# Gathering 14 columns a layer for fewer partitions, with VectorE filling in the rest

## The chip, the cores and the metric

The kernel runs on one core of a Trainium2 chip. The metric is device time in microseconds of one execution; the figure given for a kernel is the median of its runs. A profile is one execution of its own, taken by the hardware profiler, and its times are its own.

## What is computed

A graph with 6250 nodes and 100,000 edges (sorted by destination) goes through two GATv2 layers and one GAT layer, each followed by what the listing shows; features are 256 wide. In all three, a node gathers one row from each of its sources, turns them to logits, takes a softmax over its own edges and adds up the weighted rows.

```python
def _gatv2_layer(x, src, dst, n, Wl, Wr, att, b):      # H, C = 4, 64; edges have self-loops added
    xl = (x @ Wl).reshape(n, H, C)
    xr = (x @ Wr).reshape(n, H, C)
    e = leaky_relu(xl[src] + xr[dst], 0.2)
    logits = einsum('ehc,hc->eh', e, att)
    alpha = segment_softmax(logits, dst)
    out = segment_sum(xl[src] * alpha[:, :, None], dst, num_segments=n)
    return out.reshape(n, H * C) + b

h = elu(_gatv2_layer(x, ..., first weights))
x = layernorm(x + _gatv2_layer(h, ..., second weights))
Wh = einsum('nf,hfd->hnd', x, W)                       # 8 heads of 32
e = leaky_relu(s1[:, src] + s2[:, dst], 0.2)
attn = segment_softmax(e, dst)
x = layernorm(x + segment_sum(attn[:, :, None] * Wh[:, src], dst))
```

(`segment_softmax` stands for the maximum, exponential, sum and division that the reference writes out.)

## The kernel before

**Plan.** `make_plan` (L715) counts each node's edges, sorts the nodes by that number, most first, and cuts them into 49 blocks of 128 nodes, one node to a partition. Node r of the order is partition r mod 128 of block r // 128. `columns` (L46) works out from the sizes alone how many columns each block gets: `cols` is 38 for block 0 (27 of them held in the block, the rest by a special path called "few"), then 25, 24, 23, 22, 21, 21, 20 and so on down to 9 for block 48, such that a node of block b has more than `cols[b]` edges only with a chance that is neglected. `near` holds for each node the list of its sources, with a place NP for "no source" where the list is shorter than the columns; row NP of each table has logits of -1.5e38 or rows that lead to them (`nobody`). The tile `most` (L926) holds the number of columns of each block; L1163 compares the counts with it, and a graph that doesn't fit goes by `tile_general_path` (L81), a slower program in the same kernel. The rows of layer 1's table are written by the plan as well.

**Layers.** `tile_by_degree` (L1208) does the three layers. `layer2` (L1536) is called twice for the GATv2 layers, and the GAT layer stands open at the end (from L1758). For each block, in order:

- `gather_rows` (L1295) issues one indirect DMA from GpSimd's queue for each column: 128 rows of the table, one to a partition, by the indices of that column (L1300). They land in tiles `g` of at most 9 columns. There are 9 such tiles (L1266), and a block takes two or three, four at block 0. In layers 1 and 2 column 0 of a block's tiles is the node's own row and comes from elsewhere.
- `attend` (L1576) has VectorE take the maximum with the own right-hand row `xr` (L1591, or `first_z` at L1567 for the first tile of the next block), the product with the attention vector (L1594) and the sum over each head (L1595), which gives `lg`. `weights` (L1434) takes VectorE's maximum over the columns (L1439), ScalarE's exponential with its sum (L1446), and VectorE's division (L1451, L1452).
- `weighted_sum` (L1464) multiplies the gathered rows by the weights, most columns on VectorE (L1483) and the last ones on ScalarE (L1482), and lets TensorE add the columns up into `acc` (L1490).
- `finish1` and `finish2` make the next layer's rows and write them (L1708, L1709, L1740).
- In layer 3 `attend` (L1771) adds two numbers per edge (L1782), VectorE multiplies all columns by their weights (L1503) and adds them up (L1512), and the finished rows are scattered by GpSimd (L1812).

The program of each engine is written out in order by hand (no scheduler): for block b the gathers of block b+1 are issued first, then b+1's own rows are made ready, then `attend(b)`, then the finish of b-1 and the weighted sum of b.

**From one layer to the next.** `begin` (L1382) starts the next layer's gathers early: the first 14, 12 and 11 columns of blocks 0, 1 and 2 (`EARLY`), from indices in `soon`, as soon as the rows of blocks 0 to 44 of the new table are written. `sort_sources` (L1388) has put those blocks' sources in order in layer 1.

Of the kernel before, what the change touches and what calls it, by code (L numbers as in the profile page):

```python
# [35 lines left out]
P = 128  # L36
BIG = 1.5e38
SLOPE = 0.2
EPS = 1e-5
FAR = 1 << 20  # L40
RUNS = 64
EARLY = (14, 12, 11)
LATE = 4


def columns(E, N, NB):  # L46

    mean = E / N
    pmf = [math.exp(-mean)]
    for k in range(1, 200):
        pmf.append(pmf[-1] * mean / k)
    over, sd = [], []
    for c in range(199):
        p = sum(pmf[c + 1 :])
        g = sum((k - mean) * pmf[k] for k in range(c + 1, 200))
        over.append(N * p)  # L60
        sd.append(math.sqrt(max(N * (p * (1.0 - p) - g * g / mean), 0.0)))
    cols = []
    for b in range(NB):
        most = P * b
        cols.append(next(
            c for c in range(199) if (over[c] + 3.5 * sd[c] <= most if b else over[c] < 0.01)
        ))
    low = max((c for c in range(199) if N - over[c] <= P // 4), default=0)
    high = next(c for c in range(199) if over[c] <= P // 4)
    pmf += [0.0] * 200  # L70
    held = next(
        c for c in range(199)
        if N * sum((k - c) * pmf[k] for k in range(c, 200))
        + 3.5 * math.sqrt(N * sum((k - c) ** 2 * pmf[k] for k in range(c, 200))) <= P
    )
    assert cols[1] <= held < cols[0]
    return cols, low, high, held


@with_exitstack  # L80
# [565 lines left out]
@with_exitstack  # L646
def kernel(
    ctx: ExitStack,
    tc: tile.TileContext,
    x: bass.AP,  # L650
    src: bass.AP,
    dst: bass.AP,
    wl1: bass.AP,
    wr1: bass.AP,
    att1: bass.AP,
    b1: bass.AP,
    wl2: bass.AP,
    wr2: bass.AP,
    att2: bass.AP,
    b2: bass.AP,  # L660
    w3: bass.AP,
    a3: bass.AP,
    out: bass.AP,
):
    nc = tc.nc
    N, F = x.shape
    E = src.shape[0]
    NB = -(-N // P)
    NP = NB * P
    cols, low, high, held = columns(E, N, NB)  # L670
    CM = max(cols)
    H2, D2 = att1.shape
    H1 = w3.shape[0]
    W2 = H2 * (D2 + 1)

    dram = ctx.enter_context(tc.tile_pool(name="plan_dram", bufs=1, space=DRAM))
    plan = ctx.enter_context(tc.tile_pool(name="plan", bufs=1))
    node_i = plan.tile([P, NB], I32, name="node_i")
    fits = plan.tile([P, 1], I32, name="fits")
    done = plan.tile([P, 1], I32, name="done")  # L680
    ident = plan.tile([P, P], F32, name="ident")
    eps = plan.tile([P, 1], F32, name="eps")
    nobody = plan.tile([1, 2, max(W2 + 1, F + H1)], F32, name="nobody")
    att = [plan.tile([P, H2, D2 + 1], F32, name=f"att_r{i}") for i in range(2)]
    wc = [plan.tile([P, 2, 2, H2, D2 + 1], F32, name=f"wcat{i}") for i in range(2)]
    wh = plan.tile([P, 2, F + 2 * H1], F32, name="wh_cat")
    fixed = plan.tile([P, 4, F], F32, name="fixed_r")
    xl1_d = dram.tile([NP + 1, W2 + 1], F32, name="xl1_d")
    near_d = dram.tile([NP, CM + F], F32, name="near_d")

    with tc.manual_schedule():
        make_plan(
            tc, x, src, dst, ((wl1, wr1, att1), (wl2, wr2, att2)), (b1, b2), w3, a3,
            cols, low, high, held, node_i, fits, ident, eps, nobody, att, wc, wh, fixed, xl1_d, near_d,
        )
        nc.vector.memset(done, 0)

    att = [t.rearrange("p h d -> p (h d)") for t in att]
    wc = [w.rearrange("p j c h d -> p j c (h d)") for w in wc]
    ok = nc.values_load(fits[0:1, 0:1], min_val=0, max_val=1)  # L700
    with tc.If(ok != 0):
        with tc.manual_schedule():
            tile_by_degree(
                tc, x, att1, b1, b2, w3, a3, out, [held] + cols[1:], node_i, near_d, ident, eps, nobody,
                xl1_d, att, wc, wh, fixed, done,
            )
    right = nc.values_load(done[0:1, 0:1], min_val=0, max_val=1)
    with tc.If(right == 0):
        tile_general_path(
            tc, x, src, dst, wl1, wr1, att1, b1, wl2, wr2, att2, b2, w3, a3, out,  # L710
        )
# [1 line left out]

@with_exitstack
def make_plan(  # L715
    ctx, tc, x, src, dst, layers, biases, w3, a3, cols, low, high, held, node_i, fits, ident, eps, nobody,
    att, wc, wh, fixed, xl1_d, near_d,
):


# [1 line left out]
    nc = tc.nc  # L722
# [205 lines left out]
    for b in range(1, NB + 1):  # L928
        if b == NB or cols[b] != cols[b0]:
            nc.gpsimd.memset(most[:, b0:b], float(cols[b0]))  # L930
            b0 = b

# [271 lines left out]

@with_exitstack
def tile_by_degree(  # L1208
    ctx, tc, x, att1, b1, b2, w3, a3, out, cols, node_i, near_d, ident, eps, nobody,
    xl1_d, att, wc, wh, fixed, done,  # L1210
):
    nc = tc.nc
# [76 lines left out]
    def node(b):  # L1289
        return bass.IndirectOffsetOnAxis(ap=node_i[:, b : b + 1], axis=0)  # L1290

    def source(of, b, j):
        return bass.IndirectOffsetOnAxis(ap=of[:, b, j : j + 1], axis=0)

    def gather_rows(b, rows, cut, own, table, of, width, j0, j1):  # L1295


        for g, (s0, s1) in zip(rows, cut):
            for j in range(max(s0 - own, j0), min(s1 - own, j1)):
                nc.gpsimd.indirect_dma_start(  # L1300
                    out=g[:, j + own - s0, :width], out_offset=None, in_=table,
                    in_offset=source(of, b, j),
                )

    def find_few(work, ps):

# [229 lines left out]
    def layer2(i, table, of, width, start, own, finish, follow):  # L1536
# [5 lines left out]
        with ExitStack() as es:  # L1542
# [24 lines left out]
            def first_z(b):  # L1567
                rows, cut, xr = state[b]
                n = cut[0][1]
                z = zp.tile([P, T, W2], F32, name="z")[:, :n, :]  # L1570
                nc.vector.tensor_max(  # L1571
                    z, rows[0][:, :n, :W2], xr[:, None, :].to_broadcast([P, n, W2])
                )
                state[b].append(z)

            def attend(b):  # L1576
                rows, cut, xr, *made = state.pop(b)
                S = cols[b] + 1
                lg = work.tile([P, CM + 1, H2], F32, name="lg")
                if b == 0:  # L1580
                    own_r = work.tile([P, W2], F32, name="few_own", bufs=1)
                    nc.scalar.copy(own_r, xr)
                    po = pst.tile([P, W2], F32, name="few_r", tag="tp")
                    nc.tensor.matmul(po, node_of, own_r, start=True, stop=True)
                for g, (s0, s1) in zip(rows, cut):
                    n = s1 - s0
                    if s0 == 0 and made:
                        z = made[0]
                    else:
                        z = zp.tile([P, T, W2], F32, name="z")[:, :n, :]  # L1590
                        nc.vector.tensor_max(  # L1591
                            z, g[:, :n, :W2], xr[:, None, :].to_broadcast([P, n, W2])
                        )
                    nc.vector.tensor_mul(z, z, at[:, None, :].to_broadcast([P, n, W2]))  # L1594
                    nc.vector.reduce_sum(  # L1595
                        lg[:, s0:s1, :], z.rearrange("p t (h d) -> p t h d", h=H2), axis=AX.X
                    )
                if b == 0:
                    none(po)
                    z = zp.tile([P, T, W2], F32, name="z")[:, 0, :]  # L1600
                    nc.vector.tensor_max(z, few_row[:, :W2], po)
                    nc.vector.tensor_mul(z, z, at)
                    few_lg = work.tile([P, H2], F32, name="few_lg", bufs=1)
                    nc.vector.reduce_sum(few_lg, per_head(z, H2), axis=AX.X)
                    few_logits(work, pst, lg, few_lg, H2)
                    if i == 0:
                        nc.vector.tensor_copy(few_at[:, 1:], few_row[:, W2 : W2 + 1])
# [150 lines left out]
    with ExitStack() as es:  # L1758
# [12 lines left out]
        def attend(b):  # L1771
# [3 lines left out]
            if b == 0:  # L1775
                few_logits(work, ps, lg, few_row[:, F:A1], H1)
                nc.vector.tensor_add(
                    lg[:, cols[0] :, :], lg[:, cols[0] :, :],
                    s2[:, :1, :].to_broadcast([P, FEW, H1]),
                )  # L1780
            for g, (s0, s1) in zip(rows, cut):
                nc.vector.tensor_add(  # L1782
                    lg[:, s0:s1, :], g[:, : s1 - s0, F:A1],
                    s2[:, b : b + 1, :].to_broadcast([P, s1 - s0, H1]),
                )
            nc.vector.scalar_tensor_tensor(
                lg[:, :S, :], lg[:, :S, :], SLOPE, lg[:, :S, :], op0=OP.mult, op1=OP.max
            )
# [84 lines left out]
```

## Time and profile before

| | us |
|---|---|
| median of 3 runs | 3332.04 |
| lowest and highest of them | 3331.96, 3335.03 |
| the profiled execution, as timed | 3328.12 |
| its span in the profile | 3326.3 |
| VectorE busy | 2755.3 |
| GpSimd busy | 2435.2 |
| TensorE matmuls, weight loads busy | 1416.2, 1131.0 |
| ScalarE busy | 1108.0 |

The profile has 24,261 instructions in this span. The stages, read from its timeline: the plan until the first row gather at 131.25 us, layer 1 until VectorE's first product of layer 2 at 1261.70, layer 2 until its last row is written (issued at 2278.5), with layer 3's early gathers from 2235.97, then layer 3. The mean granted clock of TensorE is 0.711 of full speed.

How to read it: "busy" leaves out the time in which an engine's queue issues or waits, so that an engine can be full below 100%. A timeline row has the start, the duration, the engine, the line, the operation, the tile written and the tiles read, and, in brackets, how long the engine stood idle before it and what ended that; "issue" means that the profile shows nothing that it waited for. A group's row has its busy time and the mean duration in ns, then the idle time before its instructions. A row of waits has the total, the number and the longest. Rows by stretch have busy time and instruction count of each engine.

### The profile page before, as it was taken

The page shows a single profiled execution, that of the slowest core. Times are in us where ns is not written, and L with a number is a line of the kernel's source. Part 1 is how long each engine was busy: PE and PEld are TensorE (multiplying, and loading weights), DVE is VectorE, ACT ScalarE, POOL GpSimd, SP SyncE. Part 2 cuts the span into 40 slices and gives each one's busy share as a digit, 9 for nine tenths or more (in the row PEclk, how much of TensorE's full clock was granted, in tenths as well). Part 3 has the DMA queues.
Part 4 walks back from the last instruction along what each step waited for, and adds up shares of the span by engine and source line. Part 5 has one row for each costly group of instructions (what it writes and reads, how often), then busy time and mean ns, then how long its engine had stood idle before and what let it go on. Part 6 is the DMA issues. An engine that isn't in the chain of part 4 may idle for free.

```text
span 3326.3 us, 24261 instructions
## 1 busy us (share of the span) xinstructions
PE 1416.2 (43%) x5423; PEld 1131.0 (34%) x5424; DVE 2755.3 (83%) x2527; ACT 1108.0 (33%) x4428; POOL 2435.2 (73%) x2588
## 2 busy tenths in 40 slices
PE   7346666666677773565656666662000000000000
PEld 5235554555555552454545454552000000000000
DVE  7599998889888888999999999985966767666766
ACT  3134434444444442444445666561000000000000
POOL 5477777777777767777777777767777777777776
PEclk8678888888888886777877878886555555555555
DMA  8744444444444444444444444444333333333333
GB/s 198 145 111 118 117 118 121 118 120 122 121 121 121 124 111 112 122 121 127 121 127 126 132 126 132 131 111 115 108 107 107 108 108 107 108 107 107 107 107 86
DMA packets 189103, 395.84 MB, mean 119 GB/s; under 512 B 56249, under 2 KB 107963, under 8 KB 188934
## 3 DMA queue, kind: packets, MB, share of 16 engines
q0 software_dynamic: 121392, 339.19, 39.0%
q1 hardware_dynamic: 59858, 53.27, 5.7%
q10 hardware_dynamic: 7700, 1.74, 0.5%
q8 instruction: 47, 0.77, 0.1%
q14 instruction: 106, 0.87, 0.1%
HBM read 354.02 MB, written 40.42 MB: 119 GB/s over the span
## 4 chain that ended last, share of the span: by engine, by line
POOL 23%; DVE 15%; issue 13%; PE 7%; DMA 3%; ACT 1%; DVEq 0%; POOLq 0%; ACTq 0%
POOL g L1300 22%; PE acc L1490 6%; DVE g L1483 3%; DVE z L1594 3%; DVE lg L1595 3%; DVE z L1571 3%; DVE z L1591 2%; DMA g<-xl_d,near_r 1%; POOL out L1812 1%; DMA out<-y,node_i 1%; PE pm L1427 1%; DVE stats L1522 0%; DMA g<-whs_d,near_r 0%; ACT sd L1526 0%; DVE weighted L1503 0%
## 5 line engine op out<-in xcount | busy, mean ns | idle before, releaser
L1300 POOL DMA_INDIRECT g<-xl_d,near_r x1569 | 1484.4, 946 | 485.8 <-issue 434.8
L1490 PE MATMUL acc<-g,ident 128*128 128x256 f32 x3408 | 972.0, 455 | 654.2 <-DVE g L1483 357.6
L1490 PEld LDWEIGHTS acc<-g,ident 128*128 128x128 f32 x3408 | 788.8, 235 | 838.3 <-DVE g L1483 378.4
L1300 POOL DMA_INDIRECT g<-whs_d,near_r x766 | 727.1, 949 | 233.3 <-issue 227.2
L1482 ACT ACTIVATE g<-g,by 128x64 f32<-128x64 f32 x2308 | 561.0, 336 | 1.6
L1595 DVE TENSOR_REDUCE lg<-z 128x28 f32<-128x1820 f32 (+4 forms) x234 | 497.4, 2125 | 8.1
L1594 DVE TENSOR_TENSOR z<-z,at 128x1820 f32<-128x1820 f32 (+4 forms) x234 | 496.9, 2124 | 4.7
L1483 DVE TENSOR_TENSOR g<-g,wt 128x1792 f32<-128x1792 f32 (+8 forms) x234 | 331.8, 1435 | 31.9 <-ACT by L1473 31.9
L1512 DVE TENSOR_REDUCE acc_v<-weighted 128x256 f32<-128x4096 f32 (+15 forms) x49 | 343.7, 7014 | 1.6
L1591 DVE TENSOR_TENSOR z<-g,pr 128x1820 f32<-128x1820 f32 (+3 forms) x138 | 299.6, 2171 | 23.2 <-DMA g<-xl_d,near_r 14.8
L1456 ACT ACTIVATE wt<-lg 128x128 f32<-128x128 f32 (+17 forms) x49 | 14.0, 285 | 803.6 <-DVE lg L1455 803.6
L1782 DVE TENSOR_TENSOR lg<-g,s_r 128x56 f32<-128x56 f32 (+4 forms) x111 | 22.4, 214 | 268.5 <-DMA g<-whs_d,near_r 212.2
L1571 DVE TENSOR_TENSOR z<-g,pr 128x2080 f32<-128x2080 f32 (+4 forms) x96 | 197.9, 2061 | 44.5 <-DMA g<-xl_d,near_r 13.5
L1503 DVE TENSOR_TENSOR weighted<-g,wt 128x1792 f32<-128x1792 f32 (+4 forms) x111 | 226.6, 2057 | 0.1
L1422 ACT COPY xT<-pt 128x256 f32<-128x256 f32 x147 | 55.0, 374 | 505.8 <-PE pt L1420 505.8
L1446 ACT ACTIVATE wt<-lg,top 128x19 f32<-128x19 f32 (+14 forms) x392 | 115.7, 295 | 234.2 <-DVE top L1439 224.7
L1427 PE MATMUL pm<-wcat,xT 128*128 128x260 f32 x392 | 99.0, 395 | 22.6 <-ACT xT L1422 22.6
L1427 PEld LDWEIGHTS pm<-wcat,xT 128*128 128x128 f32 x392 | 70.4, 189 | 42.8 <-ACT xT L1422 34.3
L1446 ACT ACTIVATION_READ_ACCUMULATOR wt<-lg,top 128x1 f32 x392 | 73.5, 187 | 0.0
L1812 POOL DMA_INDIRECT out<-y,node_i x49 | 50.1, 1022 | 25.8 <-issue 14.2
L1427 PE MATMUL pm<-wh_cat,xT 128*128 128x272 f32 x196 | 59.0, 424 | 22.6 <-ACT xT L1422 22.6
L1427 PE MATMUL pl<-wcat,xT 128*128 128x260 f32 x196 | 57.2, 415 | 25.2 <-ACT xT L1422 25.2
(250 smaller groups left out, 1527.3 us busy)
## 6 DMA issues: line engine op xcount, KB each, us to landing
g<-xl_d,near_r POOLq DMA_INDIRECT x1569, 2.8
g<-whs_d,near_r POOLq DMA_INDIRECT x766, 2.8
whs_d<-row SPq DMA_DIRECT2D x49, 132.0 KB, 2.0
xl_d<-xl SPq DMA_DIRECT2D x49, 130.0 KB, 7.9
xl_d<-row SPq DMA_DIRECT2D x49, 130.0 KB, 2.6
xr_d<-row SPq DMA_DIRECT2D x49, 130.0 KB, 2.9
two<-xl_d SPq DMA_DIRECT2D x49, 130.0 KB, 2.9
two<-xr_d SPq DMA_DIRECT2D x49, 130.0 KB, 3.3
```

The source lines that it names most:

```text
L1300: nc.gpsimd.indirect_dma_start(out=g[:, j + own - s0, :width], out_offset=None, in_=table, in_offset=source(of, b, j),)
L1427: nc.tensor.matmul(pm, xT[:, c, :], w[:, c, :], start=c == 0, stop=c == 1)
L1446: nc.scalar.activation(wt[:, :, h], lg[:, :S, h], AF.Exp, bias=top[:, h : h + 1], accum_out=den[:, h : h + 1],)
L1482: nc.scalar.mul(g4[:, t, h, :], g4[:, t, h, :], by[:, t - m, h : h + 1])
L1483: nc.vector.tensor_mul(g4[:, :m], g4[:, :m], wt[:, s0 : s0 + m, :].unsqueeze(3).to_broadcast([P, m, H, F // H]),)
L1490: nc.tensor.matmul(acc, ident, g4[:, t], start=False, stop=s0 + t == S - 1 and not more)
L1503: nc.vector.tensor_mul(prod[:, s0 - base : s1 - base, :].rearrange("p t (h d) -> p t h d", h=H), g[:, :n, :F].rearrange("p t (h d) -> p t ...
L1512: nc.vector.reduce_sum(part, prod[:, : s1 - base, :].rearrange("p s f -> p f s"), axis=AX.X)
L1571: nc.vector.tensor_max(z, rows[0][:, :n, :W2], xr[:, None, :].to_broadcast([P, n, W2]))
L1591: nc.vector.tensor_max(z, g[:, :n, :W2], xr[:, None, :].to_broadcast([P, n, W2]))
L1594: nc.vector.tensor_mul(z, z, at[:, None, :].to_broadcast([P, n, W2]))
L1595: nc.vector.reduce_sum(lg[:, s0:s1, :], z.rearrange("p t (h d) -> p t h d", h=H2), axis=AX.X)
```

## The change

For each column c of a block b from 1 on, the same statistic that sets `cols` bounds how many nodes of the block can have more than c edges. Where that bound, rounded up to a multiple of 32, is 32, 64 or 96, the column is "short". There are 14 such columns: (block, column: rows) 1, 24: 64; 2, 23: 32; 3, 22: 64; 13, 18: 32; 17, 17: 64; 26, 15: 96; 31, 14: 96; 36, 13: 32; 40, 12: 32; 43, 11: 32; 45, 10: 96; 47, 9: 32; 48, 7: 96; 48, 8: 32. All but the first of block 48's are the last column of their block.

A short column is gathered for its first n partitions only. At the start of `attend(b)` VectorE writes zeros to the other partitions of that column of `g`, and after the logits are made it writes -1.5e38 to their logits. Partitions 32 to 127 take two such writes (32 to 63, and 64 to 127), partitions from 64 or from 96 on take one. In layer 1 blocks 0 to 2 are left as they were, since their columns also carry the sources that `sort_sources` needs; the early gathers use no short column. In the plan GpSimd writes the lower limits into `most` for those partitions, so that the comparison at L1163 covers them.

```diff
+QUARTER = 32
...
+    short = {}
+    for b in range(1, NB):
+        for c in range(cols[b]):
+            most = math.ceil((over[c] + 3.5 * sd[c] - P * b) / QUARTER) * QUARTER
+            if QUARTER <= most < P:
+                short[b, c] = most
+    return cols, low, high, held, short
+
+def past(n):
+    return ([(QUARTER, 2 * QUARTER)] if n == QUARTER else []) + [(max(n, 2 * QUARTER), P)]
...
+    for (b, c), n in sorted(short.items(), key=lambda e: -e[0][1]):
+        for p0, p1 in past(n):
+            nc.gpsimd.memset(most[p0:p1, b : b + 1], float(c))
...
     def gather_rows(b, rows, cut, own, table, of, width, j0, j1):
         for g, (s0, s1) in zip(rows, cut):
             for j in range(max(s0 - own, j0), min(s1 - own, j1)):
+                n = rows_of(b, j, width)
                 nc.gpsimd.indirect_dma_start(
-                    out=g[:, j + own - s0, :width], out_offset=None, in_=table,
-                    in_offset=source(of, b, j),
+                    out=g[:n, j + own - s0, :width], out_offset=None, in_=table,
+                    in_offset=bass.IndirectOffsetOnAxis(ap=of[:n, b, j : j + 1], axis=0),
                 )
+    def rows_of(b, j, width):
+        return P if width == W2 + 1 and b < len(EARLY) else short.get((b, j), P)
+
+    def empty(b, own, width, rows, cut):
+        parts = []
+        for g, (s0, s1) in zip(rows, cut):
+            for s in range(max(s0, own), s1):
+                n = rows_of(b, s - own, width)
+                for p0, p1 in past(n) if n < P else []:
+                    nc.vector.memset(g[p0:p1, s - s0, :width], 0.0)
+                    parts.append((p0, p1, s))
+        return parts
+
+    def hopeless(lg, parts):
+        for p0, p1, s in parts:
+            nc.vector.memset(lg[p0:p1, s : s + 1, :], -BIG)
...
                 lg = work.tile([P, CM + 1, H2], F32, name="lg")
+                parts = empty(b, 1, width, rows, cut)
...
                     nc.vector.reduce_sum(
                         lg[:, s0:s1, :], z.rearrange("p t (h d) -> p t h d", h=H2), axis=AX.X
                     )
+                hopeless(lg, parts)
...
+            parts = empty(b, 0, A1, rows, cut)
             for g, (s0, s1) in zip(rows, cut):
                 nc.vector.tensor_add(
                     lg[:, s0:s1, :], g[:, : s1 - s0, F:A1],
                     s2[:, b : b + 1, :].to_broadcast([P, s1 - s0, H1]),
                 )
+            hopeless(lg, parts)
```

More of the change, by code (lines that the diff above doesn't have):

```diff
@@ L76, in columns @@
     assert cols[1] <= held < cols[0]
-    return cols, low, high, held
+    short = {}
[7 more added lines that the diff above has]
+    return ([(QUARTER, 2 * QUARTER)] if n == QUARTER else []) + [(max(n, 2 * QUARTER), P)]
 @with_exitstack
@@ L669 @@
     NP = NB * P
-    cols, low, high, held = columns(E, N, NB)
+    cols, low, high, held, short = columns(E, N, NB)
     CM = max(cols)
@@ L693 @@
             tc, x, src, dst, ((wl1, wr1, att1), (wl2, wr2, att2)), (b1, b2), w3, a3,
-            cols, low, high, held, node_i, fits, ident, eps, nobody, att, wc, wh, fixed, xl1_d, near_d,
+            cols, low, high, held, short, node_i, fits, ident, eps, nobody, att, wc, wh, fixed, xl1_d,
+            near_d,
         )
@@ L703 @@
             tile_by_degree(
-                tc, x, att1, b1, b2, w3, a3, out, [held] + cols[1:], node_i, near_d, ident, eps, nobody,
+                tc, x, att1, b1, b2, w3, a3, out, [held] + cols[1:], short, node_i, near_d, ident, eps, nobody,
                 xl1_d, att, wc, wh, fixed, done,
@@ L715, in make_plan @@
 def make_plan(
-    ctx, tc, x, src, dst, layers, biases, w3, a3, cols, low, high, held, node_i, fits, ident, eps, nobody,
-    att, wc, wh, fixed, xl1_d, near_d,
+    ctx, tc, x, src, dst, layers, biases, w3, a3, cols, low, high, held, short, node_i, fits, ident, eps,
+    nobody, att, wc, wh, fixed, xl1_d, near_d,
 ):
@@ L1208, in tile_by_degree @@
 def tile_by_degree(
-    ctx, tc, x, att1, b1, b2, w3, a3, out, cols, node_i, near_d, ident, eps, nobody,
+    ctx, tc, x, att1, b1, b2, w3, a3, out, cols, short, node_i, near_d, ident, eps, nobody,
     xl1_d, att, wc, wh, fixed, done,
@@ L1290, in node @@
         return bass.IndirectOffsetOnAxis(ap=node_i[:, b : b + 1], axis=0)
-    def source(of, b, j):
-        return bass.IndirectOffsetOnAxis(ap=of[:, b, j : j + 1], axis=0)
     def gather_rows(b, rows, cut, own, table, of, width, j0, j1):
@@ L1569, in first_z @@
                 n = cut[0][1]
+                assert all(rows_of(b, s - 1, width) == P for s in range(1, n))
                 z = zp.tile([P, T, W2], F32, name="z")[:, :n, :]
```

## The prediction

> **What bounds the kernel now.** I read the shares of busy time first.
>
> ```profile
> PE 1416.2 (43%) x5423; PEld 1131.0 (34%) x5424; DVE 2755.3 (83%) x2527; ACT 1108.0 (33%) x4428; POOL 2435.2 (73%) x2588
> ```
>
> GpSimd looks freer than VectorE, but its gap between gathers is not free time. The groups by line give 0.95 us a gather, and the timeline of GpSimd in layer 3 shows 0.30 us ahead of each that no other engine ends:
>
> ```profile
> L1300 POOL DMA_INDIRECT g<-whs_d,near_r x766 | 727.1, 949 | 233.3 <-issue 227.2
> ...
> 2475.71 0.98 POOL L1300 DMA_INDIRECT g<-whs_d,near_r  x1 [0.30 <-issue]
> 2476.99 0.95 POOL L1300 DMA_INDIRECT g<-whs_d,near_r  x1 [0.30 <-issue]
> 2478.24 0.95 POOL L1300 DMA_INDIRECT g<-whs_d,near_r  x1 [0.30 <-issue]
> ```
>
> One gather each 1.25 us is thus a full queue. So I read busy time by stretch (PE, PEld, DVE, ACT, POOL busy; clock; DMA), one stretch a layer:
>
> ```profile
> 500.00:700.00 200.00, 127.26 (x490) 102.16 (x490) 175.80 (x139) 88.05 (x362) 151.28 (x161) 0.85 0.45 120
> 1500.00:1700.00 200.00, 113.34 (x417) 91.65 (x418) 193.88 (x158) 87.28 (x360) 151.23 (x160) 0.79 0.46 125
> 2500.00:2700.00 200.00, 0.00 (x0) 0.00 (x0) 135.69 (x136) 11.25 (x33) 151.57 (x160) 0.50 0.40 107
> ```
>
> 160 gathers in 200 us, everywhere: GpSimd is full in all three layers. Whether it is the bound is told by VectorE's waits: 300 to 1190 us (layer 1), 1300 to 1700 (layer 2), 2270 to the end (layer 3):
>
> ```profile
> DVE pr L1671 <- PE pr L1427: 49.2, 27, 3.4
> DVE z L1591 <- DMA g<-xl_d,near_r: 7.5, 7, 1.8
> DVE z L1571 <- DMA g<-xl_d,near_r: 6.5, 11, 2.0
> ...
> DVE g L1483 <- ACT by L1473: 5.0, 16, 0.3
> DVE z L1571 <- issue: 0.3, 1, 0.3
> ...
> DVE lg L1782 <- DMA g<-whs_d,near_r: 212.2, 36, 9.3
> ```
>
> - **Layer 3** waits for gathers: GpSimd is its bound.
> - **Layer 2** never waits for one there. I counted its gathers from the first and set each tile's last landing against VectorE's read of it: block 7's last gather leaves GpSimd at 1446.5, and its tile is read at 1472.9. From block 1 on the data lie ready 11 us or more ahead. Its bound is VectorE, which from about block 18 on also waits for ScalarE's copy of the own row (L1725).
> - **Layer 1** changes over. From block 9 to 27 (407 to 839 us) a block's first rows land 0.1 to 0.8 us ahead of the read at most blocks, with waits on several (a lead of up to 8 us, won over blocks 1 to 8, is spent by block 9); from 28 on GpSimd runs ahead, to 38 us at block 48, and VectorE waits each time for TensorE's own-row product (L1671).
>
> **The change, part by part.** The instruction order of the two kernels gives 40 shorter gathers (12, 14 and 14), 60 more VectorE memsets on `g`, 60 on `lg`, 21 on GpSimd for `most`; TensorE, ScalarE and SyncE are untouched, and no gather has another wait.
>
> *Gathers.* A column cut to 32, 64 or 96 rows drops 3/4, 1/2 or 1/4 of a gather's rows. Per layer seven are cut to 32, three to 64, four to 96: 7 x 0.75 + 3 x 0.5 + 4 x 0.25 = 7.75 gathers' worth of rows. Every gather of the trace has 128 rows, so what rows cost is bounded. [...] At most all of the 0.95 goes with rows; at least nothing. In between stands the direct DMA of GpSimd, L1143 (minimum/median/maximum):
>
> ```profile
> L1143 POOL DMA_DIRECT2D near_d<-moved x6: 782/998/1064, 100.3 to 105.3; - x6
> ```
>
> Its last issue writes 512 runs (0.78 us), the others 1152 (1.00): 0.22 us for 640 runs, so 0.61 us do not go with runs. If a gather has that same fixed part, 0.95 - 0.61 = 0.34 us go with its 128 rows. I take 0.34, the one row with two sizes on this engine; ends 0 and 0.95. The 0.30 us of issue is alike before gathers, scatters and 532-byte rows, so it stays.
> - Layer 3, all on the path: 7.75 x 0.34 = -2.6 us (0 to -7.4).
> - Layer 1: only blocks 3, 13, 17 and 26 lie where GpSimd binds, or, block 3, where its time is felt from block 9 on: 0.5 + 0.75 + 0.5 + 0.25 = 2 gathers, -0.7 us (0 to -1.9). Later ones only lengthen GpSimd's lead.
> - Layer 2: 0. The saving lengthens a lead of 11 us.
>
> The Trainium skill speaks against the gain: DMA: Bandwidth & Descriptors, section "Anatomy of one DMA — SWDGE (gpsimd) path", holds descriptor generation to be a small part of the fixed cost, many descriptors coming before the increment shows. By it the first two terms would be 0, and the sum below +6.0; no row here has a gather under 128 rows to settle it.
>
> *Memsets on `g`* (260 to 264 elements, before the block's first product). VectorE's memsets in the trace are narrow:
>
> ```profile
> L1671 DVE MEMSET row<- 128x4 f32 x49 | 3.0, 62 | 0.0
> ...
> L1392 DVE MEMSET keys<- x3: 85/85/85, 213.0 to 274.6; 128x32 f32 x3
> ```
>
> 23 ns for 28 elements is 0.82 ns each; 62 + 256 x 0.82 = 0.27, and at the 1.04 ns an element of L1594 (271 ns from 1560 to 1820) 0.33. I take 0.29. *Memsets on `lg`* stand between the last reduction and the maximum, each of which needs the one ahead: 0.06 + 0.04 gap = 0.10, a second one 0.03. So a column of 64 or 96 rows (one pair) costs 0.39 us, of 32 rows (two pairs) 0.58 + 0.13 = 0.71. The high end: if each `g` memset and the instruction behind it start only when the one ahead has ended. Dependent VectorE instructions start 0.04 us after the end of the one ahead (L1282 to L1283), independent ones 0.07 before it (L1483 to L1697): 0.11 a start, two for one pair, three for two: 0.61 and 1.04.
> - Layer 2. Blocks 1, 3, 17, 26, 31 (one pair) and 2, 13 (two) have nothing over them: 5 x 0.39 + 2 x 0.71 = 3.4. Block 36 hides 0.5 in ScalarE's copy, leaving 0.2; 40, 43, 45, 47 are covered (waits 0.7 to 1.9). Behind the memsets queue the product, maximum, weights, and so TensorE and every later block. Blocks 46 to 48 do not count: layer 3's first gather waits for block 44's row (issued 2233.3), after which GpSimd is full over the boundary, and the last row (issued 2278.5, 2.0 to land) is there 1.4 us before the gather that needs it. Together +3.6; all held, 5 x 0.61 + 2 x 1.04 + 0.54 = +5.7. No row is nearer to one end: I take +4.6.
> - Layer 1. Blocks 3 to 26 are hidden by the gather ahead (if GpSimd were faster, they would cost as in layer 2), later ones by the wait for `pr`, except block 48, which has no successor: three and three, 0.87 + 0.16 = +1.0, held 1.5; layer 2's gathers wait for its row (2.53 us idle at 1260.69). I take +1.2.
> - Layer 3. `g` memsets lie in waits for gathers (212 us); `lg` ones too, except the last block's: +0.2.
>
> The Trainium skill (VectorE: DVE Perf Modes, "Two Vector instructions with no wait between them") states that an instruction whose output starts in another 32-partition group than the last one's waits until all earlier ones end. By it the held prices hold and the sum is +4.1; no instruction in this trace starts VectorE off partition 0.
>
> *GpSimd's 21 memsets* on `most`: 18 such took 0.67 us, so 0.8 us, in its idle 18 us before L1016. Without that idle time they would cost that 0.8. Bytes: 22 gathers' worth in all, under 3 of 396 MB, with DMA busy 0.40 to 0.48: nothing.
>
> **Sum:** -2.6 - 0.7 + 4.6 + 1.2 + 0.2 = **+2.7 us**; ends -7.4 - 1.9 + 3.6 + 1.0 + 0.2 = -4.5 and 5.7 + 1.5 + 0.2 = +7.4. The profiled execution took 3328.12 (span 3326.3, 1.8 around it): 3330.8. The median of the runs is 3.9 above it, so 3334.7 stands for what runs will show.
>
> **Rivals.**
> 1. *Gathers go by rows in full.* Speaks for it: the direct DMA does slow with runs. Against: 1152 runs take hardly longer than a gather of 128. -4.5: 3327.5. Should the wide memsets also slip under other work in layer 2, another -3.6: 3323.9.
> 2. *VectorE becomes what pays, and nothing comes back.* Place: layer 2's first 32 blocks. Price: +7.4, 3339.4. It decides (slower by over 0.2%, 6.7 us, about what a measurement here can tell from no change) if memsets are held and rows cost under 0.07 us a gather (7.4 - 9.75 x 0.07). For it: zero waits in that stretch; against: the slope of L1143.
> 3. *Short gathers are slower.* 14 in layer 3 at double price: +13, with the rest 3350 or so. No row supports it.
> 4. *The change does not act.* The plan's new limits could send the run to the general path; the inputs' degrees leave at most 43 nodes where 96 are gathered and 13 where 64 are, so it does not.
>
> **Chances.** Forecast 0.60; rival 1 0.17, rival 2 0.18, rival 3 0.05. Time 3334.7. The range takes the ends, 3327.5 and 3339.4, and 1.5 us for the spread of the runs (3.1 us between them): 3326 to 3341. Faster by over 0.2% (below 3325.4) needs rival 1 with hidden memsets: 0.12, allowing for a gain in the issue time. Slower (above 3338.7): rival 2 beyond its point, rival 3, and some of the forecast's upper end: 0.24. Within: 0.64.
>
> **What would show it.** Duration of an L1300 gather of 32 rows: about 0.69 us (946 - 0.75 x 340); 0.95 or 0.24 names rival 2 or 1. VectorE's memset of 261 elements near 0.29 us. Layer 3's length (first `soon` gather to the end, 1090 us) shorter by 2.6, layer 2's (1261.7 to 2236) longer by 4.6, layer 1's changed by under 1.5. The prediction is wrong if layer 2 keeps its length, or if short gathers shift the tiles' landing where VectorE waits.

## The result, and the profile after

| | before | after |
|---|---|---|
| median of the runs, us | 3333.53 (4 runs) | 3356.98 (4 runs) |
| lowest, highest, us | 3331.96, 3335.11 | 3350.28, 3357.49 |
| profiled execution: time, span, us | 3328.12, 3326.3 | 3350.28, 3348.5 |

The ratio is 1.0066, 95% interval 1.0048 to 1.0083: slower by 23.5 us, where +2.7 was forecast and 3341 was the upper end. In later runs beside other kernels, the same kernel again took 1.0067 (1.0053 to 1.0080) of the time before.

Busy time hardly tells it. The page of the changed kernel has, in place of 2755.3 us of VectorE:

```profile
PE 1417.9 (42%) x5423; PEld 1133.9 (34%) x5424; DVE 2779.4 (83%) x2647; ACT 1107.7 (33%) x4428; POOL 2436.0 (73%) x2609
```

24 us more on VectorE for 120 more instructions. The stretches shown before (busy time of PE, PEld, DVE, ACT, POOL; clock; DMA) look the same:

```profile
500.00:700.00 200.00, 128.07 (x500) 103.10 (x500) 176.90 (x144) 88.07 (x358) 151.25 (x161) 0.84 0.45 119
1500.00:1700.00 200.00, 112.64 (x431) 91.02 (x429) 194.20 (x156) 82.48 (x339) 151.24 (x161) 0.80 0.46 124
2500.00:2700.00 200.00, 0.00 (x0) 0.00 (x0) 136.31 (x137) 11.19 (x32) 151.27 (x161) 0.50 0.40 107
```

GpSimd still issues a gather each 1.25 us in all layers. VectorE's waits, in the windows used before (layer 1, layer 2, layer 3: total, times, longest), keep their kinds too:

```profile
DVE pr L1705 <- PE pr L1458: 48.5, 27, 3.6
...
DVE g L1514 <- ACT by L1504: 4.7, 15, 0.3
...
DVE lg L1817 <- DMA g<-whs_d,near_r: 214.1, 39, 9.4
```

So no bound changed hands. To find the 22.2 us between the two profiled executions, both traces were cut at the same six instructions: the maximum (`top`) of layer 1's block 0, of layer 2's blocks 0 and 48 and of layer 3's block 5, the issue of the last scatter, and the end. The table has what each piece grew by against the profiled execution of before (its own lengths in the first row), for all kernels that were run:

| kernel | plan | layer 1 | layer 2 | to layer 3, block 5 | layer 3 | ending | span |
|---|---|---|---|---|---|---|---|
| before, us | 176.4 | 1113.0 | 972.0 | 158.6 | 898.8 | 7.5 | 3326.3 |
| changed | +1.5 | +4.3 | +9.9 | 0.0 | -1.8 | +8.2 | +22.2 |
| changed, again | -0.5 | +3.9 | +6.6 | +0.2 | -1.6 | +8.3 | +16.9 |
| changed, layer 2 gathers full | +0.4 | +5.4 | +6.7 | -1.2 | -1.2 | -2.0 | +8.0 |
| writes only | -3.5 | +4.9 | +10.0 | -0.9 | +2.6 | -0.2 | +12.9 |
| writes from partition 0 | -3.4 | +9.2 | +5.1 | -0.3 | +2.3 | -0.2 | +12.7 |
| layer 2 alone | +2.1 | +4.2 | +8.7 | -1.3 | +0.6 | -1.0 | +13.3 |
| layer 3 alone | -3.0 | +0.8 | -2.8 | -0.1 | -1.4 | -1.0 | -7.3 |
| short gathers, ScalarE late | -4.6 | +2.5 | +19.4 | +0.7 | -0.1 | +8.2 | +26.2 |
| short gathers, ScalarE early | +2.2 | +2.6 | -0.6 | +2.0 | -1.2 | +8.2 | +13.2 |
| layers 1 and 3, ScalarE early | +0.7 | +3.5 | -2.7 | +0.1 | -0.4 | -2.0 | -0.8 |
| layer 1's writes on `g`, late | -2.8 | +3.9 | -2.9 | 0.0 | -0.1 | -0.2 | -2.1 |
| layer 1's writes on `g`, at start | +2.5 | +3.7 | -3.0 | 0.0 | +0.7 | +0.1 | +4.1 |
| before, more rows in layer 3 | +2.4 | -1.4 | 0.0 | +19.5 | +10.8 | +0.8 | +32.1 |

How far to trust a cell: the plan moves by -4.6 to +2.5 with no change in its loops; layer 1 by -1.4 to +4.2 and layer 2 by -3.0 to 0.0 in kernels that leave VectorE's work there as it was and put no late copy into ScalarE's. The ending counts from the last scatter's issue (the expectations count from its landing, 4.7 us before and 13.0 after); where it was taken twice for the same gathers, it repeats within 0.4 us.

Two things stand out: layer 2, and an ending that no step of the prediction had.

### The profile page after: what moved, and what is told of

It is laid out like the page before. It is cut to its first block, busy times and chain, and to the rows that moved or that the text cites. A ratio compares the mean times of both kernels' runs of the same rounds, so it can differ in the third digit from the quotient of the medians.

```text
span 3348.5 us, 24406 instructions
## 1 busy us (share of the span) xinstructions
PE 1417.9 (42%) x5423; PEld 1133.9 (34%) x5424; DVE 2779.4 (83%) x2647; ACT 1107.7 (33%) x4428; POOL 2436.0 (73%) x2609
## 5 line engine op out<-in xcount | busy, mean ns | idle before, releaser
L1848 POOL DMA_INDIRECT out<-y,node_i x49 | 50.2, 1024 | 24.9 <-issue 13.9
```

## The experiments

"Writes" are VectorE's memsets on `g` and `lg`; a one-pair column has one on each, a two-pair column two.

**Writes only.**

```diff
-                n = rows_of(b, j, width)
+                n = P
...
-                    nc.vector.memset(g[p0:p1, s - s0, :width], 0.0)
+                    nc.vector.memset(aside[p0:p1, :], 0.0)
```

> Every gather keeps its 128 rows; VectorE still makes all 120 writes of the change, at the same places and lengths, but those on g go to a scratch tile (the ones on lg stay where they are and write what is there already). The output is the reference's. Theory A (VectorE pays: one write pair 0.62 us, two pairs 1.07 us in layer 2, as read from the changed kernel's trace, and only part of it hidden in layer 1; the longer ending of the run, 13.0 us from the last scatter's landing to the end of the span against 4.7 before, belongs to the short gathers): layer 2 longer by 9 to 11 us, layer 1 by 2 to 4, layer 3 the same within 1, ending 4.7; time +12 to +16 over the kernel before. Theory B (short gathers disturb what follows, and the writes are mostly hidden): time +3 or less, layer 2 within 3 us of before.

3341.58 us, +12.9, ratio 1.0042 (1.0028 to 1.0056): theory A. At the maxima of layer 2's blocks 1, 2, 3, 13, 17, 26 this kernel falls behind by 0.61, 1.06, 0.60, 1.07, 0.61, 0.62 us, the changed kernel by 0.61, 1.08, 0.62, 1.07, 0.62, 0.62, and blocks 4 to 11 by nothing in both. So in these blocks the writes are the whole cost, short gathers none of it. Layer 1 grew by 4.9, not by 2 to 4. Layer 3 grew by 2.6, not by under 1: 2.1 of it are GpSimd's gathers (729.2 us for 766 of them against 727.1), for which no run shows a cause.

**Writes from partition 0.** As above, but `aside[: p1 - p0, :]`, and the writes on `lg` go aside in the same way.

> As the kernel with the writes only, but all 120 VectorE writes go to the scratch tile and start at partition 0, with the same number of partitions and elements as before. Theory A1 (what makes a pair cost 0.62 and not 0.39 us in layer 2 is the start at partition 32, 64 or 96, with each write waiting for the instruction ahead and the next one for it): a pair costs 0.39, two pairs 0.71, layer 2 longer by 18 pairs' worth, 6 to 7 us instead of 10; time +8 to +10. Theory A2 (any write in between costs this, wherever it starts): the same as with the writes at their own partitions, within 1.5 us.

3338.09 us, +9.4, ratio 1.0028 (1.0017 to 1.0039). Layer 2 grew by 5.1, and in its first blocks a pair cost 0.20 to 0.22 us and two pairs 0.61: theory A1 in the main, with prices still under its 0.39 and 0.71. Not all of the drop is the partition's, though. In the changed kernel 0.12 of a pair's 0.61 is the write on `lg`: block 1's maximum starts 0.16 us after the reduction in front of it ends, and 0.03 after it before the change. From partition 0 it is 0.03 again, but there the write is on a tile that the maximum doesn't read. What is left, 0.49 against 0.20 to 0.22, is the write on `g`, on the same scratch tile in both runs. With two pairs, the second write goes over the first one there and starts 0.11 us after its end. (Its layer 1 grew by 9.2, which stays unexplained.) The timeline of VectorE at layer 2's block 13 (two pairs) shows why (start, duration, engine, line, operation). Before:

```profile
1603.98 2.35 DVE L1483 TENSOR_TENSOR g<-g,wt 128x1792 f32<-128x1792 f32 x2
1606.24 1.77 DVE L1594 TENSOR_TENSOR z<-z,at 128x1560 f32<-128x1560 f32 x1
```

The changed kernel:

```profile
1611.70 2.34 DVE L1514 TENSOR_TENSOR g<-g,wt 128x1792 f32<-128x1792 f32 x2
1614.15 0.64 DVE L1328 MEMSET g<- 32x260 f32 x2
1614.80 1.78 DVE L1627 TENSOR_TENSOR z<-z,at 128x1560 f32<-128x1560 f32 x1
```

From partition 0:

```profile
1610.53 2.34 DVE L1515 TENSOR_TENSOR g<-g,wt 128x1792 f32<-128x1792 f32 x2
1612.86 0.66 DVE L1329 MEMSET wh_prod<- 32x256 f32 x2
1613.44 1.71 DVE L1628 TENSOR_TENSOR z<-z,at 128x1560 f32<-128x1560 f32 x1
```

Before, the next product starts 0.09 us ahead of the end of the one in front (1606.33). In the changed kernel the first write starts 0.11 us after that end, and the product after the last write's end. With the writes only, on the scratch tile at their own partitions, the first one at this block starts 0.10 us after that end (1609.76 against 1609.66), and the product again after the last write's end. From partition 0 the write starts at the end of the one in front, and the product 0.08 ahead of the write's.

**Layer 3 alone.** `rows_of` gives 128 unless `width == A1`.

> The change in layer 3 alone: 14 short gathers and their VectorE writes there, layers 1 and 2 as before the change. Theory A: layers 1 and 2 unchanged within 1 us, layer 3 shorter by 2 to 3 us; ending 13.0 if any short gather is enough, 4.7 + 8.3 x 14/40 = 7.6 if it goes with their number: time +5.5 or about +0.5; -2.5 if the ending has another cause. Theory B: layer 3 not shorter, layers 1 and 2 unchanged.

3325.90 us, ratio 0.9992 (0.9983 to 1.0001); layer 3 is 1.4 us shorter and the ending, at 6.5, shorter than before rather than longer. Neither length guessed for it held; the time, 2.8 us below before, is near the -2.5 given for an ending with another cause. That led to theory C below.

**Short gathers, ScalarE late.** VectorE writes nothing; ScalarE copies a "no source" row into the partitions that are not gathered, after its part of the weighted sum.

```diff
-                    nc.vector.memset(g[p0:p1, s - s0, :width], 0.0)
+                    nc.scalar.copy(g[p0:p1, s - s0, :width], nobody[p0:p1, int(width == A1), :width])
```

> Short gathers as in the change, but VectorE makes no write at all: ScalarE copies a 'no source' row (zeros and -1.5e38) into the partitions not gathered, right after its part of the weighted sum, where the trace of before shows it idle for some 4 us; the logits then come out as -1.5e38 without a write on lg. Theory A: layers 1 and 2 within 1 us of before, layer 3 shorter by 2 to 3 us, ending 13.0 instead of 4.7: time +5 to +6.5. If the longer ending is not due to the short gathers: time -2 to -3. Theory B: layer 2 stays longer by 9 to 10 us and the time is +14 or more.

3357.01 us, +28.3, ratio 1.0086 (1.0073 to 1.0100): by the number theory B, and neither by the trace. Up to layer 2's block 18 little is lost (0.5 us up to block 4, then -0.2; a kernel with full gathers in this layer, layers 1 and 3 alone, loses 0.35 at block 3 too). Then each block with a copy, 26 to 47, loses 2.5 to 3.9 us. ScalarE and VectorE at block 26:

```profile
1875.80 7.78 ACT L1506 ACTIVATE g<-g,by 128x64 f32<-128x64 f32 x32
1883.61 0.41 ACT L1327 COPY g<-nobody 32x260 f32<-32x260 f32 x1
```

```profile
1877.84 2.32 DVE L1620 TENSOR_REDUCE lg<-z 128x32 f32<-128x2080 f32 x1
1884.05 2.59 DVE L1616 TENSOR_TENSOR z<-g,pr 128x2340 f32<-128x2340 f32 x1 [3.89 <-ACT g L1327]
```

The copy stands behind 7.78 us of multiplications, and VectorE waits 3.89 us for it: the place, not the short gather.

**Short gathers, ScalarE early.** The copies moved into `between`, ahead of those multiplications.

> Short gathers in all three layers, no VectorE write; ScalarE's copies of the 'no source' row now stand right after its copy of the weights (ahead of its part of the weighted sum), where it idles 2.5 us for VectorE in layer 2, and no longer behind 7.8 us of multiplications that end after VectorE wants the tile. Theory A (what cost layer 2 in the previous ScalarE kernel was the late copy, not the short gathers): layers 1 and 2 within 1 us of before from block 0 to 48, layer 3 shorter by 2 to 3 us; the ending as in the changed kernel (last two steps of GpSimd 2.42 and 9.05 us, against 0.77 and 2.27): time +5 to +7 over before. Theory B (short gathers disturb layer 2): layer 2 longer by 5 us or more, time +12 or more.

3341.35 us, +10.4, ratio 1.0033 (1.0020 to 1.0045). Layer 2 is back within 1 us (-0.6), inside the -3.0 to 0.0 of kernels that leave it alone, so no disturbance by short gathers shows there; of the +10.4 the ending is 8.2. The expected +5 to +7 was missed by the 2.6 of layer 1 and the 2.0 after layer 2, which these runs don't explain.

**Layers 1 and 3, ScalarE early.** Layer 2 gathers 128 rows.

> The same with short gathers in layers 1 and 3 only: 1760 rows fewer are gathered than before. Theory C (the ending goes with the number of rows gathered by the whole run, 0.575 ns a row from the kernel with 992 rows fewer, 1.70 us for the last step against 2.27, and jumps up once the count passes a boundary between 992 and 2752 rows fewer): the last two steps take 0.52 and 1.26 us, or, past the boundary, 2.5 and 9.6. Time: -4 to -5 in the first case, +4.5 in the second. Theory D (it goes with something else about short gathers): 0.77 and 2.27, or values between.

3327.40 us, ratio 0.9989 (0.9980 to 0.9998): the one version that beats both kernels, by 3.6 us. Its last two steps took 0.38 and 0.80 us: theory C. (832 rows go in layer 1 and 992 in each of the others, so "1760" and "2752" in the expectations should read 1824 and 2816. Their 0.77, 2.42 and so on for the first step hold 0.03 us of an earlier one of its kind.)

**More rows.**

```diff
+            if 0 < b <= 8:
+                gather_rows(b, rows, cut, 0, wh_d[:, :], spots, A1, cols[b] - 1, cols[b])
```

> The kernel before with 8 more gathers of 128 rows in layer 3: the last column of blocks 1 to 8 is gathered a second time, with the same rows. Time +10 or so for 8 gathers of 1.25 us. Theory C: 1024 rows more make the last two steps 0.92 and 2.86 us. Theory D (only short gathers change the ending): 0.77 and 2.27.

3360.20 us in its one run, with 30 us (not 10) more up to block 9 of layer 3: each of the 8 repeated gathers waited 2.1 to 3.4 us, for the first one into the same place to land. The last two steps took 0.90 and 2.93 us: theory C.

**Layer 2 alone.** `rows_of` gives 128 unless `width == W2`.

> The change in layer 2 alone, with its VectorE writes: 14 short gathers there, layers 1 and 3 as before. Theory A: layer 2 longer by 9 to 11 us from block 0 to 48, every pair of writes 0.62 us and two pairs 1.07 up to block 31, layer 1 as before (395 us from block 27 to 48, where the runs with writes in layer 1 had 399 and those without 394 to 396), layer 3 as before. Theory C: 992 rows fewer, so the ending as in the kernel with the change in layer 3 alone, 0.63 and 1.70 us. Time +8 to +10. Rival: the writes are hidden in layer 2 when layer 1 doesn't come first with its own delays; then +3 or less.

3338.97 us, +8.0, ratio 1.0020 (1.0010 to 1.0029); layer 2 +8.7, the last two steps 0.56 and 1.54 us. Theory A again, and near enough to C.

**Layer 2 gathers full, all else as changed**, and the changed kernel beside it on the same chip.

```diff
-                n = rows_of(b, j, width)
+                n = P if width == W2 else rows_of(b, j, width)
...
-                    nc.vector.memset(g[p0:p1, s - s0, :width], 0.0)
+                    nc.vector.memset(aside[p0:p1, :] if width == W2 else g[p0:p1, s - s0, :width], 0.0)
```

> The changed kernel, except that layer 2 gathers all 128 rows everywhere; its VectorE writes stay, those on g of layer 2 going to a scratch tile, so that VectorE's work is the same. 1760 rows fewer than before are gathered, instead of 2752. Theory C (the ending goes with the number of rows): the last two steps of GpSimd take 0.4 and 0.8 us instead of 2.42 and 9.05, and the run is 10 to 10.5 us shorter than the changed kernel, 12 to 14 longer than before. Rival (the ending goes with short gathers in layers 1 and 2, however many): the ending stays, and the time with it.

> The changed kernel itself, on the same chip as the one with full gathers in layer 2. Both theories: 21 to 25 us over the kernel before; the ending 2.42 and 9.05; layer 1 from block 27 to 48 399 us, layer 2 from block 0 to 31 698.6 and from 32 to 48 265.9, if these repeat from run to run.

3337.88 against 3349.26 us: 11.4 us come back when 992 rows *more* are gathered. The ratios to before are 1.0031 (1.0019 to 1.0043) and 1.0067 (1.0053 to 1.0080). VectorE's writes are the same, layers 1 to 3 differ by 0.1 to 1.5 us. The last two steps of GpSimd, in the instructions by line (count, minimum/median/maximum in ns, first and last start), before:

```profile
L708 POOLq INC_SWDGE_SEM  x1: 740/740/740, 3322.4 to 3322.4; - x1
...
L1869 POOLq DRAIN  x3: 50/107/2273, 3323.2 to 3326.0; - x3
```

changed:

```profile
L720 POOLq INC_SWDGE_SEM  x1: 2395/2395/2395, 3336.2 to 3336.2; - x1
...
L1905 POOLq DRAIN  x3: 50/102/9052, 3338.6 to 3348.2; - x3
```

layer 2 gathers full:

```profile
L720 POOLq INC_SWDGE_SEM  x1: 380/380/380, 3332.2 to 3332.2; - x1
...
L1906 POOLq DRAIN  x3: 50/102/803, 3332.7 to 3334.0; - x3
```

**Where layer 1's writes stand.** Full gathers; of the writes only those meant for `g` in layer 1 (on the scratch tile), none at block 48: once right before VectorE's wait for `pr`, once at the start of the block.

> All gathers full; of the writes only those on g in layer 1 (scratch tile), moved from the start of the block's work to the place right before VectorE waits for TensorE's own-row product of the next block; none at block 48. Theory E (the writes of layer 1's late blocks are covered by that wait, and the 4 us that they cost at the block's start come from TensorE's sums falling into slower stretches of its clock): a cost that has nothing to do with their 0.28 us each, from 0 to +5 us between blocks 27 and 48 (394 to 400), with the matmul sums of these blocks going the same way as the length. Theory F (there is no slack, every write lengthens the block): +3 to +4 us, with the matmul sums as in the runs without writes (166.5 to 169.3 us).

> As the kernel with layer 1's writes before the wait, but they stand at the start of the block's work, where the change has them; still none on lg and none at block 48. Theory E1 (it is the place: a later start of the products and of the exponential shifts the matmul sums): blocks 27 to 48 take 398 to 400 us and the matmul sums 171 to 172. Theory E2 (it is the writes on lg and the three pairs of block 48, which has no wait behind it): 394 to 396.5 us and 166.5 to 169.3.

3327.85 us, ratio 0.9999 (0.9990 to 1.0008), and 3331.02, ratio 1.0000 (0.9991 to 1.0010). From the maximum of block 27 to that of 48 it took 395.8 and 395.9 us, and the matmul sums (the spacings of the matmuls that add up a block's columns, over these blocks) were 167.9 and 168.0: both in the range of kernels without writes, 393.6 to 396.0 and 166.5 to 169.3. A two-pair column ahead of the wait, in VectorE's timeline of the first:

```profile
1156.89 0.25 DVE L1471 TENSOR_REDUCE top<-lg 128x4 f32<-128x52 f32 x1
1157.24 0.64 DVE L1329 MEMSET wh_prod<- 32x256 f32 x2
1159.05 0.06 DVE L1705 MEMSET pr<- 128x4 f32 x1 [1.17 <-PE pr L1459]
```

1.17 us of wait are left after 0.64 us of writes: covered, wherever they stand (theory E2). In the four kernels with all of layer 1's writes as changed, these blocks took 398.9 to 399.9 us and the matmul sums 171.5 to 172.1. So it comes with the writes on `lg` or with block 48. The maximum of block 47 lies ahead of block 48's writes, and up to it the four took 383.1 to 384.1 us, the two here 380.5 and 381.4, kernels without VectorE writes in layer 1 378.3 to 381.5. So most of it is there before block 48, which points to the writes on `lg`; no run has these alone. How much of it is TensorE's clock was not separated.

## Why the prediction was wrong

- **The ending, +8.2 of +22.2: no step had it.** The sum is added to "3328.12 (span 3326.3, 1.8 around it)" and has no term for what follows the last scatter, so it put that at nothing without a reason. After the last scatter GpSimd runs two closing steps (`INC_SWDGE_SEM` and the longest `DRAIN`); they took 0.74 + 2.27 us before and 2.40 + 9.05 after. The run with full gathers in layer 2 shows that the gathered rows set them.
- **"Block 36 hides 0.5 [...] 40, 43, 45, 47 are covered", and layer 2's +4.6.** Layer 2 grew by 9.9 (6.6, 8.7 in other profiles). From block 0 to 31 the kernels with the writes at their own partitions took 697.8 to 699.0 us, those without VectorE writes and without late copies 692.8 to 694.2: 4.9 between the means, near the upper end for these blocks (5 x 0.61 + 2 x 1.04 = 5.1), not the 3.4 of the lower one nor a value between. From 32 to 48 it is 263.4 to 265.9 against 258.1 to 261.4: 5.3 between the means, where 0.2 was taken. In the profile of before itself this stretch is 261.3, the longest but one without writes, so against it alone the growth is 2.1 to 4.6. The cover is real block by block (43 loses 1.02 and 44 gains 1.09; 45 loses 0.60, 46 gains 0.62), but not for blocks 47 and 48, which lose 1.07 and 0.47. "Blocks 46 to 48 do not count" failed too in the changed kernel: it is no nearer to before at layer 3's block 5 (0.0, +0.2), though three other kernels with the same writes in layer 2 gave back 0.9 to 1.3 on the way. The rest of what this stretch lost no run explains.
- **"0.34 us go with its 128 rows."** In the changed kernel a gather of 128 rows takes 946 ns at the median, of 96 rows 922, of 64 rows 910, of 32 rows 873: (946 - 873)/96 = 0.76 ns a row, 0.10 us for 128. So 0.85 us of a gather, not 0.61, don't go with its rows: the direct DMA's fixed part did not carry over. A gather saves 0.07 at most, where the sum took up to 0.75 x 0.34 = 0.26. GpSimd's last gathers in the changed kernel (two columns of block 48: 96 rows, then 32) in its timeline:

```profile
3314.88 0.95 POOL L1313 DMA_INDIRECT g<-whs_d,near_r  x1 [0.30 <-issue]
3316.13 0.92 POOL L1313 DMA_INDIRECT g<-whs_d,near_r  x1 [0.30 <-issue]
3317.36 0.86 POOL L1313 DMA_INDIRECT g<-whs_d,near_r  x1 [0.30 <-issue]
```

- **Layer 3, -2.4: right in sign, for another reason.** It shrank by 1.8 and 1.6 us. The issue of 14 gathers gave 7 x 0.07 + 3 x 0.04 + 4 x 0.02 = 0.7, some 0.5 of it by the 11 that lie behind block 3. The larger part is the last gather of all, for which the sum had no term: its 32 rows landed 2.35 us after issue, where the 128 of before took 3.68 (2.3 to 2.7 in other kernels that cut it, 3.7 to 3.9 in those that don't), and only then does the last block start (VectorE's addition of its logits begins 0.02 us after that landing before, 0.08 after the change).
- **Layer 1, -0.7 + 1.2: not resolved as a whole.** +4.3 and +3.9, with -1.4 to +4.2 in kernels that leave this layer's VectorE work alone. That the writes on `g` slip under the wait for `pr` was right. That all later writes but block 48's do was not: from block 27 to 47 the kernels with all of them took 1.6 us or more longer than any without.
- **The writes themselves were right:** 275 to 278 ns where 0.29 us was taken, in the groups by line (busy us, mean ns, idle before):

```profile
L1328 DVE MEMSET g<- 32x264 f32 x11 | 3.1, 278 | 1.0
L1328 DVE MEMSET g<- 32x260 f32 x11 | 3.0, 275 | 1.2
```

 and the held prices 0.61 and 1.04 measured 0.62 and 1.07. Choosing a value between 3.6 and 5.7 because "no row is nearer to one end" was the error: the rule on 32-partition groups in the Trainium skill (VectorE: DVE Perf Modes, "Two Vector instructions with no wait between them") gave the upper end, and the run from partition 0 agrees with it (0.20 to 0.22 us for the write on `g` in place of 0.49). Its other rule (DMA: Bandwidth & Descriptors, "Anatomy of one DMA — SWDGE (gpsimd) path"), that many descriptors can be emitted before the incremental cost shows, agrees with 0.10 us of 0.95 for 128 rows.
- **`most`:** the plan moved by +1.5 and -0.5, within its spread.

Rival 2 named the mechanism (VectorE pays, nothing comes back) and stopped at +7.4, as beyond layer 2's block 32 it too counted block 36 alone, and it had no ending.

## What to carry to other kernels

Before cutting the rows of a gather, read what a gather costs per instruction and what per row: here 0.85 us of 0.95 and the 0.30 of issue went with the instruction, so cutting rows gave little back (fewer gathers were not tried). A write that fills the rest is cheap only in a stretch where its engine waits, or on an engine that is idle there, at a place ahead of its long work; if it stands in the bound engine's stream, count each write and the instruction behind it as starting only after the one ahead has ended, and start it at partition 0 if the layout allows (tried here only as a scratch write). And compare the two traces to the very last instruction: a term that nobody listed can sit after the work is done.

## What the runs showed of the hardware

GpSimd's two closing steps follow the rows that the run gathered, down to the nanosecond the same in kernels with the same gathers:

| rows gathered, against before | kernels | first step, us | second step, us |
|---|---|---|---|
| +1024 | more rows | 0.90 | 2.93 |
| 0 | before and four with full gathers | 0.74 | 2.27 |
| -992 | layer 3 alone; layer 2 alone | 0.60; 0.56 | 1.70; 1.54 |
| -1824 | two | 0.38 | 0.80 |
| -2816 | changed (twice), and two with ScalarE | 2.40 | 9.05 |

Against before, the second step falls by 0.6 to 0.8 ns a row and the first by 0.1 to 0.2, and both jump somewhere between 1824 and 2816 rows fewer. That looks like a count that starts anew, but no run shows what is counted, or why layers 2 and 3 differ by 0.16 us in the second step at the same number of rows; so the number of rows alone does not set them.
